# A graph layer on one core: 128 single rows a block, addressed by byte offsets that VectorE works out, and ranges of 38 nodes

## The chip, the cores and the metric

The kernel runs on one core of a Trainium2 chip. The metric is the time of one execution on the device, in microseconds; the time before is the median of three runs, 15436.6 us (15436.29 to 15437.57). The engines are named as the profile names them: PE multiplies matrices (PEld loads its weights), DVE is VectorE, ACT is ScalarE, POOL is GpSimd, SP is SyncE. SP, ACT and POOL also have queues from which transfers (DMAs) are issued.

## What is computed

There are 50000 nodes with 128 numbers each (x), and 1650000 edges (src, dst) sorted by their target dst. Each edge has type 0 or 1. Every node also has an edge to itself. The reference, cut to what matters:

```python
src, dst = (edge_index[0], edge_index[1])
Xs = X[src]
m_data = Xs @ W_data.T + b_data
m_ctrl = Xs @ W_control.T + b_control
msg = jnp.where((edge_types == 0)[:, None], m_data, m_ctrl)
agg = jax.ops.segment_sum(msg, dst, num_segments=X.shape[0])
out = agg + (X @ W_self.T + b_self)
return jax.nn.relu(out)
# around it: x = layernorm(x + the above)
```

So for each edge the row of its source is fetched, and the rows are summed per target and type. The weights can be applied after the sums.

## The kernel before

The edges are cut into blocks. A block is Q = 4 steps, and a step has R = 7 chunks of CH = 128 edges and F = 22 edges more; behind the four steps stand X = 96 edges. A block therefore holds BE = 28 x 128 + 4 x 22 + 96 = 3768 edges, and there are NBLK = 438 blocks. Ten blocks (GB) form a group, for which `load_edges` (line 106) loads the edge lists.

The rows of the sources come in three ways:

- Chunks. Each of the 28 chunks of a block is one gather issued from POOL (line 408): an indirect DMA that fetches 128 rows of x by 128 indices. Its target is one of 70 buffers (`gat`). DVE works out the indices in `fill`, five blocks ahead.
- Left-out edges. The edges of nodes to themselves need no gather, since a window of 128 rows of x is loaded per block anyway (`window`). `fill` takes 22 of them out of each step and puts the 22 extra edges in their places in the chunks, so these ride along. The `left_out` functions add the rows that were taken out.
- Single rows. The X last edges of a block are fetched one by one, each by a DMA of 512 bytes. `single_rows` (line 383) issues a quarter of them after each step: half from SP's queue, half from ACT's. The node's number is loaded from one_g into a register of the queue (line 391), and the DMA addresses x by it (line 396). This happens two blocks ahead (AHEAD); the tile yx has four buffers. All X rows together are the last, shorter chunk of the block.

For each chunk, PE multiplies the gathered rows with a matrix of zeros and ones (`oh`, built by `onehot`, line 356), which has a column for each of W = 36 nodes and two types: the range of nodes that a step may touch. The result `acc` (line 411) is added by DVE into the block's sums at a position read from a register (`add`, line 418). `counts` sums the columns of `oh` to count the edges for the biases. `take_over` (line 424) copies what the last block left for the nodes of this one, on ACT. `layer` applies the weights to the sums, `moments` and `store` do the rest; the square root of the variance is on ACT (line 446), and the result goes out on SP's queue (line 455).

The order is written out by hand (line 457 on). Within block b it is: window of b + 3, edge lists of the next group if the block is the second of its group, add of block b - 1's last step, `take_over`, `add_left_out`; then per step the products, and between them layer, moments and store of block b - 1, onehot and counts of block b + 2, fill of block b + 5, and a quarter of the single rows of block b + 2. Each engine works through its part of this in order. ACT's part is short: copy (line 427), square root (line 446), then its 48 rows.

DMAs of SP and ACT take eight semaphores in turn. Each waits until the DMA that used its semaphore before, from either queue, has landed; this wait is in the DMA instruction itself.

If a step's range were longer than W, or fewer than F edges of a step led from a node to itself, a general path (line 542) would compute everything anew.

Of the kernel before, what the change touches and what calls it, by code (L numbers as in the profile page):

```python
# [11 lines left out]
F32 = mybir.dt.float32  # L12
BF16 = mybir.dt.bfloat16
I32 = mybir.dt.int32
AF = mybir.ActivationFunctionType
ALU = mybir.AluOpType
AX = mybir.AxisListType
# [3 lines left out]

N = 50000
D = 128
E = 1650000
P = 128
EPS = 1e-5
# [3 lines left out]


R = 7
W = 36
Q = 4
B = 128
C = R * Q
X = 96
C1 = C + 1
F = 22
BE = C * CH + Q * F + X  # L40
NBLK = -(-E // BE)
REST = E - (NBLK - 1) * BE
RCH = -(-REST // CH)
LAST = REST - (RCH - 1) * CH
assert RCH <= C
GB = 10
# [7 lines left out]
U = 35  # L54
CPP = -(-(-(-E // CH) + U) // P)
NCH = CPP * P
# [11 lines left out]
def row_bcast(ap, n=P):  # L68
    return bass.AP(tensor=ap.tensor, offset=ap.offset, ap=[[0, n], *ap.ap])


def straight(ctx, tc, c, x, x_t, src_t, dst_t, etype_t, src_f, dst_f, etype_f, src_x, dst_first, out):
# [13 lines left out]
    nc = tc.nc  # L86
    keep = ctx.enter_context(tc.tile_pool(name="keep", bufs=1))
    keep_ps = ctx.enter_context(tc.tile_pool(name="keep_ps", bufs=1, space=bass.MemoryType.PSUM))
    eds = ctx.enter_context(tc.tile_pool(name="eds", bufs=2))
# [11 lines left out]
    stats = keep.tile([P, 2, 2, GROUPS], F32, name="stats")  # L101
    loops = keep.tile([P, GROUPS], F32, name="loops")

    one_s = {}

    def load_edges(g):
        t = eds.tile([1, GB * X], I32, name="one_g")
        nc.sync.dma_start(t, src_x[None, g * GB * X:(g + 1) * GB * X])
        one_s[g] = t
        loads[g] = {}  # L110
        for name, a in (("s", src_t), ("d", dst_t), ("t", etype_t)):
            t = eds.tile([P, GB, C1], I32, name=name, bufs=1)
            nc.sync.dma_start(t.rearrange("p b c -> p (b c)"), a[:, g * GC:(g + 1) * GC])
            loads[g][name] = t
        for name, a in (("sf", src_f), ("df", dst_f), ("tf", etype_f)):
            t = eds.tile([P, GB, Q, F], I32, name=name, bufs=1)
            nc.sync.dma_start(t.rearrange("p b q f -> p (b q f)"),
                              row_bcast(a[g * GB * Q * F:(g + 1) * GB * Q * F]))
            loads[g][name] = t


    load_edges(0)
    BL = TBL
    first_i = keep.tile([P, BL, Q], I32, name="first_i")
    nc.sync.dma_start(first_i.rearrange("p b q -> p (b q)"), row_bcast(dst_first))
# [5 lines left out]
    nc.vector.tensor_tensor(begin, first_i, base.to_broadcast([P, BL, Q]), op=ALU.subtract)  # L131
    nc.vector.tensor_scalar(begin, begin, 0.0, float(B - W), op0=ALU.max, op1=ALU.min)
    place_i = keep.tile([1, BL, Q], I32, name="place_i")
    nc.vector.tensor_copy(place_i, begin[0:1, :, :])
    nc.vector.tensor_tensor(begin, begin, base.to_broadcast([P, BL, Q]), op=ALU.add)
    base_i = keep.tile([1, BL], I32, name="base_i")
    nc.vector.tensor_copy(base_i, base[0:1, :, 0])
# [6 lines left out]

    num = keep.tile([P, 2 * W], F32, name="num")
    nc.gpsimd.iota(num, pattern=[[1, 2 * W]], base=0, channel_multiplier=0,
                   allow_small_or_imprecise_dtypes=True)
    FILL = Q * F + C
    small = keep_ps.tile([P, 2 * W + F + 2 * FILL + 2], F32, name="small")
    num_ps, rank_no_ps = small[:, :2 * W], small[:, 2 * W:2 * W + F]  # L150
    lists = [small[:, 2 * W + F + i * FILL:][:, :FILL] for i in range(2)]
    sums_at = [small[:Q * F, 2 * W + F + 2 * FILL + i:][:, :1] for i in range(2)]
# [16 lines left out]
    for t in range(2):  # L169
        nc.vector.memset(to_row[:, t, t:t + 1], 1.0)  # L170
    bias = keep.tile([3, D], F32, name="bias")
    for i, b in enumerate((c["b_data"], c["b_ctrl"], c["b_self"])):
# [86 lines left out]
    def fill(b):  # L259
# [19 lines left out]
        v = fil.tile([P, C], F32, name="v_new")  # L279
        nc.vector.tensor_reduce(v, new, AX.X, ALU.add)  # L280
        vi = fil.tile([P, C], I32, name="vi")
# [9 lines left out]
        with nc.allow_low_precision(reason="whole numbers below 256, one of them not 0"):  # L291
            nc.vector.tensor_reduce(by, old.rearrange("p (q r) f -> p q f r", r=R), AX.X, ALU.add)  # L292
        bys[b] = by
# [42 lines left out]
    def steps_of(b):  # L336
        return [q for q in range(Q) if len(chunks_of(b, q))]
# [4 lines left out]
    ohs, cnts, ys, accs, xws, xTs, pos, hs, mvs, sds = {}, {}, {}, {}, {}, {}, {}, {}, {}, {}  # L342

    def base_of(b):
        return nc.values_load(base_i[0:1, b:b + 1], engines=[SP], min_val=0, max_val=N - B,
                              skip_runtime_bounds_check_because="it was clamped to this")

    def window(b):
        at = base_of(b)
        xw = stp.tile([B, D], F32, name="xw", bufs=5)  # L350
        nc.sync.dma_start(xw, x[bass.ds(at, B), :])
# [12 lines left out]
    def counts(b):  # L364

        cnt = ohp.tile([P, Q, 2 * W], BF16, name="cnt")
        with nc.allow_low_precision(reason="whole numbers up to R + 1"):
            whole = [q for q in range(Q) if len(chunks_of(b, q)) == R]
            n = len(whole)
            nc.vector.tensor_reduce(cnt[:, :n, :], ohs[b][:, :n * R, :].rearrange("p (q r) w -> p q w r", r=R),  # L370
                                    AX.X, ALU.add)
            for q in steps_of(b):
# [5 lines left out]

    SHARE = X // 2
    TURN = SHARE // Q  # L380
    RANGE = dict(min_val=0, max_val=N - 1, skip_runtime_bounds_check_because="a node's number")

    def single_rows(b, q):

        if q == 0:
            ys[b] = stp.tile([X, D], F32, name="yx", bufs=AHEAD + 2)
        g, i = divmod(b, GB)
        both = []
        for j, (eng, dma) in enumerate(((SP, nc.sync), (ACT, nc.scalar))):
            at = j * SHARE + q * TURN  # L390
            _, nodes = nc.values_load_multi_w_load_instructions(
                one_s[g][0:1, i * X + at:i * X + at + TURN], engines=[eng], **RANGE)
            both.append([(dma, at + k, node) for k, node in enumerate(nodes)])
        for pair in zip(*both):
            for dma, row, node in pair:
                dma.dma_start(ys[b][row:row + 1, :], x[bass.ds(node, 1), :])  # L396

    def products(b, q):
        g, i = divmod(b, GB)
# [2 lines left out]
        for k in ks:  # L402
            if k == C:
                r, y = X, ys.pop(b)
            else:
                r = LAST if b == NBLK - 1 and k == RCH - 1 else P
                y = gat.tile([P, D], F32, name="y")
                nc.gpsimd.indirect_dma_start(  # L408
# [20 lines left out]
    def layer(b):  # L429
        a = sums[b % RING]  # L430
        po = ps_o.tile([B, D], F32, name="po")
        nc.tensor.matmul(po, xTs.pop(b), c["wselfT"], start=True, stop=False)  # L432
        nc.tensor.matmul(po, a[0:3, 2, :B], bias, start=False, stop=False)  # L433
        for t in range(2):
            nc.tensor.matmul(po, a[:, t, :B], c["wmsgT"][:, t * D:(t + 1) * D], start=False, stop=t == 1)  # L435
        pos[b] = po

    def moments(b):
# [6 lines left out]
        sd = stp.tile([B, 1], F32, name="sd")  # L445
        nc.scalar.activation(sd, mv[:, 1:2], AF.Sqrt, bias=c["eps"][:B, :])
        hs[b], mvs[b], sds[b] = h, mv, sd
# [9 lines left out]
    with tc.manual_schedule():  # L457
# [9 lines left out]
        for b in range(AHEAD):  # L467
            for q in range(Q):
                single_rows(b, q)
        left_out_numbers(0)  # L470
        left_out_rows(0)
        for b in range(NBLK + 1):
            if b + 3 < NBLK:
                window(b + 3)
            g, i = divmod(b, GB)
            if i == 1 and g + 1 < GROUPS:
                load_edges(g + 1)
# [7 lines left out]
            for q in range(Q):  # L485
                if q in qs:
                    products(b, q)
                if q == 0 and b > 0:
                    layer(b - 1)
                if q == 1:  # L490
                    left_out_numbers(b + 1)
                if q == 3:
                    left_out_columns(b + RAHEAD)
                if q in qs[:-1]:
                    add(b, q)
                if q == 0 and b > 0:
                    moments(b - 1)
                if q == 0 and b + AHEAD < NBLK:
                    onehot(b + AHEAD)
                if q == 1 and b > 0:  # L500
                    store(b - 1)
                if q == 1 and b + AHEAD < NBLK:
                    counts(b + AHEAD)
                if q == 2:
                    left_out_rows(b + 1)
                    if b + RAHEAD < NBLK:
                        fill(b + RAHEAD)
                if q == 3:
                    left_out_matrix(b + RAHEAD)
                if b + AHEAD < NBLK - 1:  # L510
                    single_rows(b + AHEAD, q)
# [20 lines left out]
    both = keep.tile([3, 1], F32, name="both")  # L532
# [9 lines left out]
def general(ctx, tc, c, x, src, dst, etype, out):  # L542
# [166 lines left out]
    with tc.For_i(0, BGROUPS, 1) as g:  # L709
# [43 lines left out]
        sd = grp.tile([NB, G], F32, name="sd")  # L753
        nc.scalar.activation(sd, mv[:, :, 1], AF.Sqrt, bias=eps[:NB, :])
        rstd = grp.tile([NB, G], F32, name="rstd")
# [8 lines left out]
def gnn_resnorm(  # L764
# [49 lines left out]
    with ExitStack() as own:  # L814
        straight(own, tc, c, x, x_t, src_t, dst_t, etype_t, src_f, dst_f, etype_f, src_x,
                 dst_first, out)
# [49 lines left out]
```

## Time and profile before

| | us |
|---|---|
| median of three runs | 15436.6 |
| profiled execution | 15434.21 |
| its span, first to last instruction | 15432.5 |
| POOL busy | 11631.9 (75%) |
| PE busy | 9551.6 (62%) |
| DVE busy | 7169.3 (46%) |
| ACT busy | 355.9 (2%) |

Busy time leaves out the instructions that set registers, wait or issue DMAs, so ACT's 2% says nothing of its queue. The profile shows the queues as ACTq and SPq. In the groups of the profile, a row gives line, engine, operation, tiles (out<-in), count, busy time, mean duration in ns, idle time before it and what ended this. In the timeline a row gives start, duration, engine, line, operation and, in brackets, the idle time before it. Of one line's instructions the profile lists the shortest, median and longest duration in ns.

### The profile page before, as it was taken

Reading aid. Unit: us, or ns where it says so; the run is one execution under the profiler, and the core shown is the slowest. Engines: PE = TensorE matmul, PEld = TensorE weight load, DVE = VectorE, ACT = ScalarE, POOL = GpSimd, SP = SyncE. Lnnn points to the kernel's source line nnn. Section 1 sums busy time; section 2 is a strip of 40 time slices with the busy share of each in tenths; the row PEclk is TensorE's granted clock in tenths of the full one; section 3 lists DMA queues with packets and bytes.
Section 4 is the critical chain, followed back from the end, with each engine's and each line's share of the span. In section 5 each row is a group of like instructions: output and inputs, shape, how many; then the busy total and the mean of one; then the engine's idle time right before and its main releaser. Section 6 shows DMA issues by size and latency. Waiting matters only on the chain.

```text
span 15432.5 us, 254222 instructions
## 1 busy us (share of the span) xinstructions
PE 9551.6 (62%) x34515; PEld 7418.5 (48%) x34516; DVE 7169.3 (46%) x12518; ACT 355.9 (2%) x881; POOL 11631.9 (75%) x12273
## 2 busy tenths in 40 slices
PE   5666666666666666666666666666666666666666
PEld 4444444444444444444444444444444444444444
DVE  5444444444444444444444444444444444444442
ACT  0000000000000000000000000000000000000000
POOL 6777777777777777777777777777777777777777
DMA  2222222222222222222222222222222222222221
GB/s 67 65 65 69 65 65 65 64 65 65 65 65 67 68 65 65 65 65 65 65 65 65 70 65 65 65 65 65 65 65 65 65 70 65 65 65 65 65 65 57
DMA packets 705933, 1008.97 MB, mean 65 GB/s; under 512 B 263521, under 2 KB 490948, under 8 KB 704222
## 3 DMA queue, kind: packets, MB, share of 16 engines
q0 software_dynamic: 392416, 804.42, 18.3%
q1 hardware_dynamic: 269416, 177.18, 4.0%
q10 hardware_dynamic: 42390, 11.02, 0.3%
q14 instruction: 1426, 11.68, 0.2%
q8 instruction: 285, 4.67, 0.1%
HBM read 962.86 MB, written 28.70 MB: 64 GB/s over the span
## 4 chain that ended last, share of the span: by engine, by line
DMA 69%; issue 11%; POOL 10%; PE 7%; DVE 2%; POOLq 0%; SPq 0%; ACTq 0%; DVEq 0%; ACT 0%
DMA y<-in_x,idx 68%; POOL y L408 10%; PE acc L411 4%; PE po L435 1%; PE po L433 1%; PE po L432 0%; POOLq L408 0%; DMA yx<-in_x 0%; SPq L396 0%; ACTq L396 0%; DVE by L292 0%; PE acc L414 0%; DMA y<-in_x,s 0%; DVE stats L198 0%; DVE stats L199 0%
## 5 line engine op out<-in xcount | busy, mean ns | idle before, releaser
L408 POOL DMA_INDIRECT y<-in_x,idx x12236 | 11605.0, 948 | 3760.9 <-DMA y<-in_x,idx 1973.1
L411 PE MATMUL acc<-oh,y 128*128 128x72 f32 x24526 | 8011.2, 446 | 5293.3 <-DMA y<-in_x,idx 5204.0
L411 PEld LDWEIGHTS acc<-oh,y 128*128 128x128 f32 x24526 | 6050.7, 315 | 7176.0 <-DMA y<-in_x,idx 6659.5
L422 DVE TENSOR_TENSOR sums<-acc,sums 128x108 f32 x1752 | 473.5, 270 | 4399.2 <-PE acc L414 4321.4
L370 DVE TENSOR_REDUCE cnt<-oh 128x216 bf16<-128x1512 f32 x438 | 1238.3, 2827 | 0.1
L360 DVE TENSOR_TENSOR oh<-col,small 128x2088 f32<-128x2088 f32 x438 | 1005.8, 2296 | 0.0
L329 DVE TENSOR_TENSOR sums<-pl,sums 128x384 f32<-128x384 f32 x437 | 243.5, 557 | 1522.8 <-ACT sums L427 1522.8
L414 PEld LDWEIGHTS <-to_row 128*128 128x128 bf16 x3504 | 639.0, 198 | 0.1
L292 DVE TENSOR_REDUCE by<-old 128x88 bf16<-128x616 f32 x437 | 583.2, 1335 | 15.1
L306 DVE COPY at<-small 88x1 f32<-88x1 f32 x437 | 67.5, 154 | 1097.9 <-PE small L299 1083.9
L440 DVE SCALAR_TENSOR_TENSOR h<-po,xw 128x128 f32<-128x128 f32 x438 | 127.5, 291 | 939.1 <-PE po L435 929.7
L435 PE MATMUL po<-wmsgT,sums 128*128 128x128 f32 x1752 | 535.3, 461 | 0.0
L375 DVE TENSOR_REDUCE cnt<-oh 128x72 bf16<-128x576 f32 x438 | 512.7, 1170 | 0.0
L427 ACT COPY sums<-sums 128x384 f32 x437 | 223.9, 512 | 12101.5 <-DMA yx<-in_x 8363.0
L414 PE MATMUL acc<-cnt,to_row 128*128 128x36 bf16 x3504 | 468.9, 217 | 0.0
L435 PEld LDWEIGHTS po<-wmsgT,sums 128*128 128x128 f32 x1752 | 406.1, 322 | 98.3 <-issue 98.3
L299 PE MATMUL small<-ones_b,by 128*88 128x1 bf16 x437 | 94.1, 215 | 493.6 <-DVE by L292 493.6
L276 DVE TENSOR_TENSOR new<-m,small 128x616 f32<-128x616 f32 x437 | 347.5, 795 | 14.9
L273 DVE TENSOR_TENSOR m<-rk,small 128x616 f32<-128x616 f32 x437 | 347.5, 795 | 14.8
L280 DVE TENSOR_REDUCE v_new<-new 128x28 f32<-128x616 f32 x437 | 347.3, 795 | 14.9
L433 PE MATMUL po<-bias,sums 3*128 3x128 f32 x876 | 346.9, 497 | 0.0
L289 DVE TENSOR_TENSOR old<-m,small 128x616 f32<-128x616 f32 x437 | 343.5, 786 | 0.1
(110 smaller groups left out, 3996.0 us busy)
## 6 DMA issues: line engine op xcount, KB each, us to landing
yx<-in_x ACTq DMA_DIRECT2D x20976, 0.5 KB
yx<-in_x SPq DMA_DIRECT2D x20976, 0.5 KB
y<-in_x,idx POOLq DMA_INDIRECT x12236
xw<-in_x SPq DMA_DIRECT2D x438, 64.0 KB
xT<-in_x_t SPq DMA_DIRECT2D x438, 64.0 KB
out<-o SPq DMA_DIRECT2D x438, 64.0 KB
sf<-in_src_f SPq DMA_DIRECT2D x44, 440.0 KB
df<-in_dst_f SPq DMA_DIRECT2D x44, 440.0 KB
```

The source lines that it names most:

```text
L273: nc.vector.tensor_tensor(m, rk_g[g][:, i, :, None].to_broadcast([P, C, F]), rank_no_ps[:, None, :].to_broadcast([P, C, F]), op=ALU.is_equal)
L276: nc.vector.tensor_tensor(new.rearrange("p (q r) f -> p q r f", r=R), m.rearrange("p (q r) f -> p q r f", r=R), vf.rearrange("p (q f) -> p ...
L292: nc.vector.tensor_reduce(by, old.rearrange("p (q r) f -> p q f r", r=R), AX.X, ALU.add)
L360: nc.vector.tensor_tensor(oh[:, :n, :], col_g[g][:, i, :n, None].to_broadcast([P, n, 2 * W]), num_ps[:, None, :].to_broadcast([P, n, 2 * W ...
L370: nc.vector.tensor_reduce(cnt[:, :n, :], ohs[b][:, :n * R, :].rearrange("p (q r) w -> p q w r", r=R), AX.X, ALU.add)
L375: nc.vector.tensor_reduce(cnt[:, q, :], ohs[b][:, k[0]:k[-1] + 1, :].rearrange("p r w -> p w r"), AX.X, ALU.add)
L408: nc.gpsimd.indirect_dma_start(out=y[:r], out_offset=None, in_=x, in_offset=bass.IndirectOffsetOnAxis(ap=idxs[b][:r, k:k + 1], axis=0))
L411: nc.tensor.matmul(acc[:, :2, :].rearrange("p t w -> p (t w)"), y[:r], ohs[b][:r, k, :], start=k == ks[0], stop=k == ks[-1])
L414: nc.tensor.matmul(acc[:, 2, :], to_row[:, t, :], cnts[b][:, q, t * W:(t + 1) * W], start=t == 0, stop=t == 1)
L422: nc.vector.tensor_tensor(part, accs.pop((b, q)), part, op=ALU.add)
L433: nc.tensor.matmul(po, a[0:3, 2, :B], bias, start=False, stop=False)
L435: nc.tensor.matmul(po, a[:, t, :B], c["wmsgT"][:, t * D:(t + 1) * D], start=False, stop=t == 1)
```

## The change

X goes from 96 to 128 and W from 36 to 38. A block then has BE = 3800 edges, and all constants that depend on it follow. The register of a single row no longer holds the node's number but the byte at which its row begins: DVE multiplies the loaded numbers by 512 (at_g), once per group, and both queues load their registers from there. The DMA sees x as one run of bytes and takes 512 from the register's offset. In the built program the queue instruction that stood ahead of each row's DMA (FUSED_REGOPS in the profile) is gone. Each queue now issues 64 rows a block, 16 after each step.

```diff
-W = 36
+W = 38
-X = 96
+X = 128
+U8 = mybir.dt.uint8
+ROW = 4 * D
...
-    one_s = {}
+    at_g = {}
 
     def load_edges(g):
         t = eds.tile([1, GB * X], I32, name="one_g")
         nc.sync.dma_start(t, src_x[None, g * GB * X:(g + 1) * GB * X])
-        one_s[g] = t
+        at = eds.tile([1, GB * X], I32, name="at_g")
+        nc.vector.tensor_scalar(at, t, float(ROW), None, op0=ALU.mult)
+        at_g[g] = at
...
-    RANGE = dict(min_val=0, max_val=N - 1, skip_runtime_bounds_check_because="a node's number")
+    RANGE = dict(min_val=0, max_val=(N - 1) * ROW, skip_runtime_bounds_check_because="where a node's row is")
+    x_bytes = x.rearrange("n d -> (n d)").bitcast(U8)[None, :]
...
-            _, nodes = nc.values_load_multi_w_load_instructions(
-                one_s[g][0:1, i * X + at:i * X + at + TURN], engines=[eng], **RANGE)
-            both.append([(dma, at + k, node) for k, node in enumerate(nodes)])
+            _, rows = nc.values_load_multi_w_load_instructions(
+                at_g[g][0:1, i * X + at:i * X + at + TURN], engines=[eng], **RANGE)
+            both.append([(dma, at + k, row) for k, row in enumerate(rows)])
         for pair in zip(*both):
-            for dma, row, node in pair:
-                dma.dma_start(ys[b][row:row + 1, :], x[bass.ds(node, 1), :])
+            for dma, k, row in pair:
+                dma.dma_start(ys[b][k:k + 1, :].bitcast(U8), x_bytes[:, bass.ds(row, ROW)])
```

## The prediction

> **What bounds the kernel now.** I read the page's chain of waits first, then the costliest groups, then the timeline of POOL, then the queues of ACT and SP, because the change moves work from POOL's gathers to those two queues.
>
> ```profile
> DMA 69%; issue 11%; POOL 10%; PE 7%; DVE 2%; POOLq 0%; SPq 0%; ACTq 0%; DVEq 0%; ACT 0%
> L408 POOL DMA_INDIRECT y<-in_x,idx x12236 | 11605.0, 948 | 3760.9 <-DMA y<-in_x,idx 1973.1
> ```
> ```profile
> 8006.06 0.94 POOL L408 DMA_INDIRECT y<-in_x,idx  x1 [0.30 <-DMA y<-in_x,idx]
> 8007.30 0.94 POOL L408 DMA_INDIRECT y<-in_x,idx  x1 [0.30 <-DMA y<-in_x,idx]
> 8008.55 0.95 POOL L408 DMA_INDIRECT y<-in_x,idx  x1 [0.30 <-DMA y<-in_x,idx]
> 8009.80 0.94 POOL L408 DMA_INDIRECT y<-in_x,idx  x1 [0.30 <-issue]
> ```
>
> The chain names the gathers' DMAs, but the timeline shows a metronome: 0.94 us of gather, 0.30 us of gap, whatever the gap is put down to. A gap that never varies is no wait. POOL issues one gather of 128 rows every 1.2486 us (mean of the undisturbed starts in the trace), and PE, DVE and the landings follow it. The first gather starts at 41.7 us, the last ends at 15413.0, and 19.5 us of tail follow. With the last block's 27 gathers there are 12263: 12263 x 1.2486 = 15312, and 199 stretched ones add 59; with 41.7 and 19.5 that is the span of 15432.5. So the number of gathers sets the time as long as nothing else is slower than a block's 28 x 1.2486 + 0.14 = 35.1 us.
>
> The candidate for "something else" is ACT's queue, which issues half of the single rows:
>
> ```profile
> 8026.30 24.25 ACTq L396 DMA_DIRECT2D yx<-in_x  x48
> 8051.37 0.51 ACT L427 COPY sums<-sums 128x384 f32 x1 [25.82 <-DMA yx<-in_x]
> 8060.16 0.29 ACT L446 ACTIVATE sd<-mv,eps 128x1 f32<-128x1 f32 x1 [8.28 <-DVE mv L444]
> 8061.21 24.10 ACTq L396 DMA_DIRECT2D yx<-in_x  x48
> 8086.17 0.51 ACT L427 COPY sums<-sums 128x384 f32 x1 [25.72 <-DMA yx<-in_x]
> ```
> ```profile
> ACT sums L427 <- DMA yx<-in_x: 8363.0, 315, 34.9
> ```
>
> ACT's block is copy, wait for DVE's moments, square root, 48 rows, copy. Nothing is idle except the 8 us before the square root, and this wait shrinks to 2.9 us (the shortest in the trace) when the copy is late. In 315 blocks of 437 the copy came right behind the rows: ACT is already the last to be ready, with a few us to spare.
>
> ```profile
> L396 ACTq FUSED_REGOPS  x20976: 37/37/37, 3.5 to 15317.2; - x200
> L396 ACTq MOVE yx<-in_x x20976: 29/29/29, 3.5 to 15317.2; - x200
> L396 ACTq DMA_DIRECT2D yx<-in_x x20976: 227/228/628, 3.6 to 15317.3; - x200
> L396 SPq DMA_DIRECT2D yx<-in_x x20976: 224/228/1187, 25.3 to 15313.8; - x200
> ```
> ```profile
> L391 ACTq TENSOR_LOAD <-one_g x1748: 773/1059/1292, 2.4 to 15311.2; - x195
> L425 ACTq TENSOR_LOAD <-shift_i x437: 287/568/752, 87.4 to 15358.8; - x146
> ```
>
> Every row costs three queue instructions: FUSED_REGOPS (node times 512), MOVE, and the DMA. Start to start that is 0.392 us on ACT and 0.41 on SP when nothing holds them (medians of the trace); the means inside a run of rows are about 0.42.
>
> **What the Trainium skill says.** "DMA: Bandwidth & Descriptors", section "SWDGE vs HWDGE vs iDMA": a gather's descriptors are written by software on GpSimd, those of DMAs from SP and ACT by hardware. The trace agrees: 944 ns of POOL for each gather, and rows that leave POOL alone. Same page, "Anatomy of one DMA": about 2.0 us of a DMA are fixed, and a wait on a semaphore is held by the issuing sequencer, not by the DMA engine. The trace shows less, 1.48 us from a row's start to its last landing (mean; 1.18 to 1.78 from 5% to 95%), and the holding. "GPSIMD Engine Reference", "Key points": GpSimd shares its SBUF interfaces with VectorE, so VectorE instructions in a two-port mode or with two SBUF inputs disturb it. The trace agrees: the stretched gathers stand beside such DVE work.
>
> ```profile
> 249.69 0.61 DVE L190 TENSOR_SCALAR col_f<-tf 128x880 f32<-128x880 int32 x1
> 250.34 1.08 DVE L191 TENSOR_TENSOR col_f<-col_f,rel_f 128x880 f32<-128x880 f32 x1
> ```
> ```profile
> 249.44 1.15 POOL L408 DMA_INDIRECT y<-in_x,idx  x1 [0.30 <-DMA y<-in_x,idx]
> 250.89 1.33 POOL L408 DMA_INDIRECT y<-in_x,idx  x1 [0.30 <-DMA y<-in_x,idx]
> ```
>
> **The change, part by part.**
>
> Fewer gathers. A block holds 28 x 128 + 4 x 22 + X edges: 3768 before, 3800 after. 1650000 edges need 438 blocks before (the last with 3384 edges, 27 chunks) and 435 after (the last with 800, 7 chunks). Gathers: 437 x 28 + 27 = 12263, then 434 x 28 + 7 = 12159. The 104 that go are worth 104 x 1.2486 = 129.9 us. The groups of ten stay 44, so the stretched gathers stay.
>
> The multiplication at_g on DVE, 1280 numbers once per group. By L190's row (880 in 0.61 us) it takes about 0.8 us. DVE is busy 7169 of 15432 us, so it costs DVE nothing; on POOL it can stretch a gather as L190 did, by 0.2 us. 43 x 0.2 = 9 us, with 0 and 0.4 us (17 us) as ends.
>
> Its wait. It stands on DVE before the last add of block b-1, and waits for one_g, which SP issues only behind its rows. In the trace before, that load lands about 5 us after this add starts in most groups (issue at 8158.41, add at 8154.08, its landing taken 2 us later, an estimate by the fixed cost in "Anatomy of one DMA"), and over 20 us after it in the first ones. Behind it on DVE stand the add, the take-over's consumer, the moments and so ACT's copy and square root; PE's layer waits for the add. None of this reaches POOL: its 70 gather buffers are 87 us of lead, and PE catches up (0.70 us for two records of a gather against 1.25). It lengthens ACT's block by 4.5 us in ten, 0.45 a block.
>
> Wider ranges. oh, cnt and the sums go from 36 to 38 columns, 5.6% of L360, L370, L375 and L422 (7.4 us a block), 0.4 us on a DVE that has 18 us free a block; PE's matmuls grow by 4 columns of 72 under gaps of half a microsecond. Nothing. In the given inputs the longest range of a step is 34 nodes, so the fallback path does not start.
>
> Rows. 64 instead of 48 per queue and block, without FUSED_REGOPS. Removing it takes 37 ns and its gap, 66 ns: 0.326 us on ACT, 0.34 on SP. But another limit is near: the rows of both queues share 8 semaphores in turn, and each DMA waits until the one 8 places earlier has landed. With rows alternating, a queue has 4 in flight: 1.48 / 4 = 0.37 us, 0.39 with the spread of the landings. Four rows after each register load start freely. ACT's block after, from the rows shown: four quarters, each with 1.63 us between the rows around a register load (1.52 measured, and 4 more registers at (1059 - 568) / 11 = 45 ns, less 66), 0.56 after the first row (0.63 less 66 ns), and 14 pitches p; less the 1.63 counted once too often; plus 1.04 to the copy, 2.9 to the square root, 1.2 to the first row, 0.45 for the new wait: 12.7 + 56 p. It reaches POOL's 35.1 at p = 0.400. With p = 0.326 it is 31.0, with three free rows and eleven at 0.388, p = 0.375, 33.7; with today's 0.434 (mean of all pitches under 0.8 us) 37.0. I take 0.375 plus 0.01 for holds by long loads, 34.3 us: under POOL's, by 0.8 us. SP has 27.4 us of work a block before (a period of 34.5 less a hold of 7.1 around 1060 us) and comes to 34 by the same pitch.
>
> Sum: 15432.5 - 129.9 + 9 = 15311.6 of span. The profiled execution took 15434.21, 1.7 more than its span, and the median is 2.4 above that: 15316 us.
>
> **Rivals.** The queues of ACT and SP become the bound, and the kernel gets slower. Place: the rows of L401; price: each 0.01 us of p above 0.400 costs 0.56 us x 434 = 243 us. At p = 0.415 it gives 15312 + 365 + 4 = 15680; if the byte offsets bring nothing, 0.434, 35.1 becomes 37.0 and the time 16140. For it: the 8 semaphores, the bursts in which the two queues wait for each other, and a DMA in bytes that may take over 228 ns. Against it: p's mean today holds waits of SP for DVE's output that vanish when ACT is late.
>
> A draw: p between 0.403 and 0.408 gives the gain back, 15436 in the middle.
>
> Gathers get dearer because a third more rows share the DMA engines: 0.011 us a gather would eat the gain. Against it: the pitch stays within 1.245 and 1.255 for 90% of the gathers, with and without rows beside them, at a DMA share of 22%. Beyond that point 15460.
>
> **How the numbers follow.** POOL stays the bound: 0.55, 15316 (15298 to 15330 by the ends above). Draw 0.10, queues over the gain 0.33, dearer gathers 0.02. This measurement tells 0.2%, 31 us, from no change. The range reaches from 15298 up to 15700, which leaves out the far half of the slow case, about 0.15, and a few hundredths below. Faster 0.55, same 0.10, slower 0.35.
>
> **What would show it.** Right: 12159 gathers at 1.249 us, no FUSED_REGOPS at the rows, ACT's rows in under 29 us a block, the wait before the square root near 3 us, at_g beside a gather of 1.15 us. Wrong: gathers with gaps of several us before which POOL waits for PE, and PE in turn for DVE or for yx; rows over 30 us a block; a row's DMA above 0.3 us; p above 0.40.

## The result, and the profile after

| | before | after |
|---|---|---|
| median of five runs each, us | 15436.6 | 15346.81 |
| lowest and highest, us | 15436.23, 15437.71 | 15330.1, 15368.69 |
| profiled execution, us | 15434.21 | 15330.1 |
| its span, us | 15432.5 | 15328.1 |
| gathers | 12263 | 12159 |

The ratio of the times is 0.9942, with a 95% interval of 0.9928 to 0.9956: 0.6% faster. The forecast was 15316 us, with a range of 15298 to 15700: of the 120.6 us forecast for the median, 89.8 came.

The page's chain of waits and two of its costliest groups, after, with the second group's row of before (line, engine, operation, tiles, count; busy time and mean ns of one; idle time before it and what ended most of it):

```profile
DMA 41%; issue 17%; ACTq 15%; PE 10%; DVE 8%; SPq 7%; POOL 1%; ACT 1%; DVEq 0%; POOLq 0%
L413 POOL DMA_INDIRECT y<-in_x,idx x12152 | 11544.6, 950 | 3737.1 <-issue 2296.8
L333 DVE TENSOR_TENSOR sums<-pl,sums 128x384 f32<-128x384 f32 x434 | 242.0, 558 | 6378.5 <-ACT sums L432 6378.5
```
```profile
L329 DVE TENSOR_TENSOR sums<-pl,sums 128x384 f32<-128x384 f32 x437 | 243.5, 557 | 1522.8 <-ACT sums L427 1522.8
```

The chain looks different: ACT's and SP's queues, at 0% before, have 22% of it, and by lines the single rows' transfers have 26% and the gathers' 10%, where the gathers' had 68% before. By the chain alone the rows would be the bound now. The gathers say otherwise; they look the same. POOL's idle time is 3737.1 / 12152 = 0.3075 us a gather, against 3760.9 / 12236 = 0.3074 before. So in the mean no gather waited longer than the constant gap, and POOL still sets the length of this execution. The row of L333 is the new fact: DVE's take-over waits 6378 us for ACT's copy, four times the 1523 us of before. ACT has come late, but POOL doesn't notice.

The timeline of ACT and its queue, after:

```profile
8042.87 30.80 ACTq L401 DMA_DIRECT2D yx<-in_x  x64
8074.48 0.51 ACT L432 COPY sums<-sums 128x384 f32 x1 [32.53 <-DMA yx<-in_x]
8076.74 0.30 ACT L451 ACTIVATE sd<-mv,eps 128x1 f32<-128x1 f32 x1 [1.75 <-DVE mv L449]
8077.97 30.87 ACTq L401 DMA_DIRECT2D yx<-in_x  x64
8109.65 0.51 ACT L432 COPY sums<-sums 128x384 f32 x1 [32.61 <-PE acc L416]
```

Copy to copy is 35.17 us, and POOL's block is 35.1. 64 rows take 30.8 us where 48 took 24.2. In 93% of the blocks the square root now follows the copy within 2.5 us, mostly at the shortest distance, 2.26 us: ACT has no slack left in its block. Its mean period over the whole execution is 35.09 us, POOL's 35.15.

The instructions of the rows, after (shortest, median and longest ns; first and last start in us):

```profile
L401 ACTq MOVE yx<-in_x x27776: 29/29/30, 6.5 to 15245.9; - x200
L401 ACTq DMA_DIRECT2D yx<-in_x x27776: 227/228/558, 6.5 to 15246.0; - x200
```
```profile
L396 ACTq TENSOR_LOAD <-at_g x1736: 1023/1297/1584, 5.2 to 15239.2; - x193
```

FUSED_REGOPS is gone from the rows, and a DMA addressed in bytes takes the same 228 ns. The median pitch of ACT's rows fell from 0.392 to 0.326 us. Loading 16 registers takes 1297 ns where 12 took 1059.

Who waits for whom, after, and PE's wait for gathers before (engine and line, what it waited for: us in total, times, longest us):

```profile
ACT sums L432 <- DMA yx<-in_x: 9724.7, 300, 36.8
DVE sums L333 <- ACT sums L432: 6378.5, 433, 22.4
...
PE acc L416 <- DMA y<-in_x,idx: 2807.7, 4989, 2.1
...
PE pl L319 <- DVE sums L333: 1724.1, 315, 15.4
```
```profile
PE acc L411 <- DMA y<-in_x,idx: 5204.0, 8983, 4.1
```

PE waited 5204 us for gathers before, 2808 us now: it comes to them later, held by DVE, which is held by ACT. That lateness is what the gather buffers take up, and they aren't used up: by the ends of PE's products and the starts of the gathers, the buffer that a gather took had been free for at least 43.6 us (before: 55.7).

Account of the span on POOL, from the starts of all gathers in the two traces:

| | us |
|---|---|
| 104 gathers fewer, at 1.2486 | -129.9 |
| stretched gathers: 199 with 59.7 us over, now 240 with 77.8 | +18.1 |
| undisturbed pitch, 1.2486 to 1.2488 | +2.6 |
| first gather later, 41.67 to 42.25 | +0.6 |
| tail behind the last gather, 19.5 to 23.7 | +4.2 |
| sum, and the difference of the spans | -104.4 |

The median of five is 16.7 us above the profiled execution, and the five spread over 38.6 us where the kernel before spread over 1.5. No trace holds that part.

### The profile page after: what moved, and what is told of

Same layout as the page of the kernel before. It is cut to its first block, busy times and chain, and to the rows that moved or that the text cites. A ratio compares the mean times of both kernels' runs of the same rounds, so it can differ in the third digit from the quotient of the medians.

```text
span 15328.1 us, 238434 instructions
## 1 busy us (share of the span) xinstructions
PE 8510.5 (56%) x34235; PEld 7111.3 (46%) x34236; DVE 7169.5 (47%) x12480; ACT 353.8 (2%) x875; POOL 11552.7 (75%) x12169
## 3 DMA queue, kind: packets, MB, share of 16 engines
q0 software_dynamic: 389088, 797.58, 20.6%
## 4 chain that ended last, share of the span: by engine, by line
DMA 41%; issue 17%; ACTq 15%; PE 10%; DVE 8%; SPq 7%; POOL 1%; ACT 1%; DVEq 0%; POOLq 0%
DMA yx<-in_x 26%; ACTq L401 11%; DMA y<-in_x,idx 10%; PE acc L416 7%; SPq L401 6%; ACTq L396 3%; DMA out<-o 2%; DMA xT<-in_x_t 1%; POOL y L413 1%; DMA xw<-in_x 1%; DVE sums L333 1%; ACT sums L432 1%; PE po L440 1%; ACTq L430 1%; PE po L438 1%
## 5 line engine op out<-in xcount | busy, mean ns | idle before, releaser
L413 POOL DMA_INDIRECT y<-in_x,idx x12152 | 11544.6, 950 | 3737.1 <-issue 2296.8
L416 PE MATMUL acc<-oh,y 128*128 128x76 f32 x24318 | 6971.0, 437 | 2855.2 <-DMA y<-in_x,idx 2807.7
L416 PEld LDWEIGHTS acc<-oh,y 128*128 128x128 f32 x24318 | 5741.7, 322 | 3939.6 <-DMA y<-in_x,idx 3730.9
L333 DVE TENSOR_TENSOR sums<-pl,sums 128x384 f32<-128x384 f32 x434 | 242.0, 558 | 6378.5 <-ACT sums L432 6378.5
L374 DVE TENSOR_REDUCE cnt<-oh 128x228 bf16<-128x1596 f32 (+1 forms) x435 | 1274.7, 2930 | 0.1
L319 PE MATMUL pl<-z,ones_b 88*128 88x256 bf16 x434 | 169.8, 391 | 1802.8 <-DVE sums L333 1724.1
L364 DVE TENSOR_TENSOR oh<-col,small 128x2204 f32<-128x2204 f32 (+1 forms) x435 | 1050.0, 2414 | 0.0
L303 PEld LDWEIGHTS <-by 128*88 128x88 bf16 x434 | 65.6, 151 | 1583.0 <-DVE by L296 1582.4
L427 DVE TENSOR_TENSOR sums<-acc,sums 128x114 f32 x1737 | 473.7, 273 | 330.9 <-PE acc L419 226.4
L296 DVE TENSOR_REDUCE by<-old 128x88 bf16<-128x616 f32 x434 | 579.3, 1335 | 14.9
L379 DVE TENSOR_REDUCE cnt<-oh 128x76 bf16<-128x608 f32 x434 | 504.5, 1162 | 0.0
L419 PE MATMUL acc<-cnt,to_row 128*128 128x38 bf16 x3474 | 473.3, 220 | 0.0
L438 PEld LDWEIGHTS po<-bias,sums 3*128 3x128 f32 x870 | 216.3, 308 | 531.5 <-DVE sums L427 443.1
```

Of the source, the lines that this page charges most:

```text
L364: nc.vector.tensor_tensor(oh[:, :n, :], col_g[g][:, i, :n, None].to_broadcast([P, n, 2 * W]), num_ps[:, None, :].to_broadcast([P, n, 2 * W ...
L379: nc.vector.tensor_reduce(cnt[:, q, :], ohs[b][:, k[0]:k[-1] + 1, :].rearrange("p r w -> p w r"), AX.X, ALU.add)
L413: nc.gpsimd.indirect_dma_start(out=y[:r], out_offset=None, in_=x, in_offset=bass.IndirectOffsetOnAxis(ap=idxs[b][:r, k:k + 1], axis=0))
L416: nc.tensor.matmul(acc[:, :2, :].rearrange("p t w -> p (t w)"), y[:r], ohs[b][:r, k, :], start=k == ks[0], stop=k == ks[-1])
L419: nc.tensor.matmul(acc[:, 2, :], to_row[:, t, :], cnts[b][:, q, t * W:(t + 1) * W], start=t == 0, stop=t == 1)
L427: nc.vector.tensor_tensor(part, accs.pop((b, q)), part, op=ALU.add)
```

## The experiments

All experiments ran on three other chips: e1 to e7 on the one numbered 11, e8 to e11 on 9, e12 on 7. There the kernel before takes 22282 to 22299 us, not 15437, so each kernel is compared only with the runs of before beside it. The times expected in e1 to e4, and the sides of e5 to e7 for a before of 15437 us, are for the first chip and can't be tested with these. What the experiments settle is how the parts of the change weigh where the queues bind. The account above rests on the two traces of the first chip; no experiment took a part of the change away there. Where Q stands in an expectation, it is the theory that the queues of SP and ACT decide; G has dearer gathers instead, and M slower memory.

| label | what differs | us | ratio to before, 95% interval | us a block |
|---|---|---|---|---|
| e1_again, e5_again | nothing (the kernel after) | 22307, 22356 | 1.003 [1.002, 1.004] | 51.4 |
| e2_one_op, e6_one_op | no copy on ACT (but in the last block) | 22759, 22767 | 1.022 [1.019, 1.024]; 1.021 [1.018, 1.023] | 52.3 |
| e3_late_mult | at_g four blocks later | 22197 | 0.996 [0.995, 0.998] | 51.0 |
| e4_by_node, e7_by_node | 128 rows, by node number | 25616, 25618 | 1.150 [1.148, 1.151]; 1.150 [1.147, 1.152] | 58.9 |
| e9_bytes_alone | 96 rows, W = 36, by byte | 19989 | 0.897 [0.895, 0.898] | 45.6 |
| e10_rows_64 | 64 rows, by byte | 18538 | 0.831 [0.830, 0.833] | 41.9 |
| e11_rows_40 | 40 rows, by byte | 18290 | 0.821 [0.819, 0.822] | 41.1 |
| e12_wide_alone | 96 rows, by node, W = 38 | 22230 | 0.998 [0.996, 0.999] | 50.8 |

The block counts for the last column are 438 with 96 rows, 435 with 128, 442 with 64 and 445 with 40. The kernel before has 22283 / 438 = 50.9 us.

### The same kernels on the other chips: e1, e5, e8

No edit: e1 and e5 are the kernel after, e8 is the kernel before.

> The changed kernel unaltered, for a second profile beside the first (15330.1 us, the fastest of its five runs of 15330 to 15369). Theory Q (the queues of ACT and SP have become a second bound, as slow a block as POOL): in a slower execution ACT's copy is further behind the block's first gather at the end than the 21 us of the first profile, by about as much as the time is longer, and POOL's pitch is the same 1.249 us. Theory G (the gathers have become dearer, the queues cost nothing): the longer time shows as more or longer stretched gathers than the 240 of the first profile, and ACT's distance at the end is the same.

> The changed kernel unaltered once more, since in the last four runs even the kernel before took 22284 us: ACT's and SP's queues show stretches there in which each instruction takes 0.7 us. Where before takes 15437 us again: 15330 to 15370 us. Theory Q (queues a second bound): ACT's copy is further behind the block's first gather at the end than the 21 us of the first profile, by about as much as the time is longer than 15330, with POOL's pitch 1.249 us. Theory G (gathers dearer): more or longer stretched gathers than 240, the same distance. Where before takes 22284 again: 22300, whatever the theory.

> The kernel before unaltered, for its profile on the chip of the last runs, where it takes 22299 us instead of 15437. Theory Q (there the queues of ACT and SP bound every kernel, before too): queue instructions of 0.7 us as in e1, POOL waiting for PE between its gathers, and PE for DVE or ACT; ACT's rows take longer than 40 us a block. Theory M (memory or gathers are slower there): POOL's gathers or the landings are longer than in the first profile of before, queue instructions are not.

Measured: 22307 us (one run), 22356 us (22320 to 22419, 14 runs) and 22264 us (one run). The gain of the first chip is gone: 0.3% slower. POOL's row in e8, the costliest groups:

```profile
L408 POOL DMA_INDIRECT y<-in_x,idx x12236 | 11603.2, 948 | 10531.7 <-PE acc L411 5573.8
```

A gather takes the same 948 ns as on the first chip, but POOL idles 10532 us instead of 3761, mostly for PE. The waits of e8 show who holds PE:

```profile
ACT sums L427 <- DMA yx<-in_x: 18655.1, 379, 193.8
DVE sums L329 <- ACT sums L427: 12135.3, 409, 51.3
...
PE pl L315 <- DVE sums L329: 10125.1, 396, 37.5
POOL y L408 <- PE acc L411: 5586.0, 1330, 17.5
```

Read upwards from the last row: POOL waits for PE (a gather buffer to come free), PE for DVE's take-over, DVE for ACT's copy, and that stands behind ACT's rows (their issue is counted in the first row). The same chain, with these names, holds in the kernel after there (e1): DVE for ACT 10540 us, PE for DVE 8827, POOL for PE 5612. This is the prediction's rival "the queues become the bound", reached already by the kernel before. Theory M finds no support: besides the gathers' 948 ns, the gathers' DMA packets of 4096 bytes last 211 ns in the median in both traces of before, and the packets that bring instructions 438 and 448. Why the queues are slow there stands in the instructions of one line, here e1's rows:

```profile
L401 ACTq MOVE yx<-in_x x27776: 2/29/1422, 6.3 to 22255.6; - x200
L401 ACTq DMA_DIRECT2D yx<-in_x x27776: 2/228/1462, 6.3 to 22255.7; - x200
L401 SPq MOVE yx<-in_x x27776: 1/29/1509, 26.0 to 22251.0; - x200
```

The medians are those of the first chip; the shortest and longest aren't. In stretches, instructions of a queue follow one another at 0.70, 1.4 or 2.1 us, whatever they are. In e1, 5263 of ACT's 27778 MOVEs and 13271 of SP's 29085 take other than 25 to 45 ns; on the first chip none does, before or after. ACT's timeline in e1 shows what it does to a block:

```profile
8053.20 45.15 ACTq L401 DMA_DIRECT2D yx<-in_x  x64
8099.16 0.51 ACT L432 COPY sums<-sums 128x384 f32 x1 [46.88 <-DMA xT<-in_x_t]
8101.42 0.29 ACT L451 ACTIVATE sd<-mv,eps 128x1 f32<-128x1 f32 x1 [1.75 <-DVE mv L449]
8102.63 33.68 ACTq L401 DMA_DIRECT2D yx<-in_x  x64
```

64 rows take 45 us in one block and 34 in the next, where the first chip has 31.

### One part alone: e4, e7, e9, e12

e4 and e7 keep the addressing by node with 128 rows and ranges of 38; e9 has the byte offsets with 96 rows and ranges of 36; e12 has only the wider ranges. Against the kernel before (e4, e12) and after (e9):

```diff
e4, e7:
-W = 36
+W = 38
-X = 96
+X = 128
e12:
-W = 36
+W = 38
e9:
-W = 38
+W = 36
-X = 128
+X = 96
```

> 128 single rows and ranges of 38 nodes, but the rows addressed by the node's number as before, with the register instruction ahead of every DMA. Theory Q: ACT's block gets longer by 0.045 us (the difference of the mean pitches, 0.434 less 0.389) to 0.066 us for each of some 60 rows, 2.5 to 4 us, and exceeds POOL's by this: 16340 to 17000 us. Theory G: the queues are off the path, and without the multiplication that stretches gathers the time is 15436.6 - 130, 15307 us.

> As e4: 128 single rows addressed by node, with the register instruction. Where before takes 15437 us, theory Q: 16340 to 17000 us (2.5 to 4 us more a block than POOL); theory G: 15307 us.

> X and W as before (96 and 36), byte offsets alone. Theory Q: from the three kernels measured where before takes 22299 us (50.9, 51.3 and 58.9 us a block with 144, 128 and 192 queue instructions for 48, 64 and 64 rows) an instruction costs 0.117 us, a row 0.148 us more and the rest of a block 27 us: 48 x (2 x 0.117 + 0.148) + 27 = 45.3 us, 438 blocks 19840 us. Theory G or M: no change but the multiplication's 18 us, 22320 us. Where before takes 15437: 15450 to 15455 us by both, from the stretched gathers.

> The kernel before with ranges of 38 nodes and nothing else: 96 rows, addressed by node. It takes the third part of the change by itself. Theory Q (the wider ranges cost nothing, as the prediction has it: their 0.4 us of DVE a block and 4 more columns a matmul lie beside the gathers on the first chip and beside the row queues here): the time of the kernel before on the same chip, ratio 0.998 to 1.002. Rival (on a chip where PE and DVE are waited for, wider tiles lie on the path: 0.4 us of DVE and 28 matmuls 4 columns wider, together 0.5 to 1 us a block of 438): 22480 to 22720 us, ratio 1.010 to 1.020. If on a chip like the first one (before at 15437 us): Q 15436, ratio 1.000.

Measured: 15.0% slower for the rows without byte offsets, 10.3% faster for byte offsets without the rows (19989 us, where theory Q had 19840), and 0.25% faster (0.15 to 0.36%) for the wider ranges alone. Per block and with 96 rows, byte offsets save 50.87 - 45.64 = 5.2 us, which is 0.11 us for each of 48 instructions taken off a queue; with 128 rows 58.9 - 51.4 = 7.5 us, 0.12 us for each of 64. An instruction and its gap cost 66 ns on the first chip. 16 more rows a queue cost 51.39 - 45.64 = 5.7 us with byte offsets and 8.0 by node number. (e5 and e9 ran on two chips, on which before differs by 0.1%.) So the change takes 5.2 us off a block there and puts 5.7 on, and the saving of three blocks in 438 (0.7%) just doesn't pay for it. POOL's row in e9, in the costliest groups, beside e8's above:

```profile
L413 POOL DMA_INDIRECT y<-in_x,idx x12236 | 11603.5, 948 | 8278.6 <-PE acc L416 3088.9
```

The same 12236 gathers with the same busy time, and 2253 us less idle time. The spans differ by 22262.1 - 19997.6 = 2264.5 us: nearly all of it is waiting that POOL no longer does. The wider ranges cost nothing that can be measured, as the prediction had it; the 52 us on the good side aren't explained.

### Less on the queues: e10, e11

The kernel after with fewer rows; nothing else is edited.

```diff
-X = 128
+X = 64
```

(and 40 in e11.)

> The changed kernel with 64 single rows a block instead of 128: 442 blocks. Theory Q where before takes 22299 us: 32 x 0.382 + 27 = 39.2 us a block, 17330 us, so fewer single rows are much faster there. Theory G or M: more gathers, hence slower than the changed kernel by 1.2%, 22620 us. Where before takes 15437: 441 x 28 + 19 = 12367 gathers, 12367 x 1.2488 + 78 + 62 = 15584 us.

> The changed kernel with 40 single rows a block: 445 blocks, 444 x 28 + 15 = 12447 gathers. Theory Q where before takes 22299 us: 20 x 0.382 + 27 = 34.6 us of queue work a block, just under POOL's 35.1, so POOL's even pitch of 1.249 us returns and the time is 12447 x 1.2488 + 78 + 62 = 15684 us, as it would be on any chip. Theory G or M: 22800 us.

Measured: 18538 and 18290 us, slower than theory Q expected by 1208 and 2606 us. Taking rows off pays less and less: 0.36 us a row and queue from 128 to 96, (45.6 - 41.9) / 16 = 0.23 from 96 to 64, (41.9 - 41.1) / 12 = 0.07 from 64 to 40. The expectations took over the first price and POOL's even pitch from the first chip. The starts of the gathers show which of them fails:

```
distance from one gather to the next:   over 5 us        2 to 5 us        under 1.3 us
before there (e8)                       439, 5192 us     1306, 3666 us     9925
by node, 128 rows (e4)                  468, 8744 us     1282, 3550 us     9924
after there (e1)                        436, 5328 us     1283, 3666 us     9898
bytes alone, 96 rows (e9)               249, 2368 us     1408, 4113 us    10021
64 rows (e10)                            72,  474 us     1419, 4232 us    10327
40 rows (e11)                            31,  203 us     1280, 3911 us    10554
```

The long pauses go with the rows: they are the waits for the queues. In e8, 434 of the 439 end 0.27 us after PE is through with the buffer that the gather takes. The short ones, some 1300 of 2 to 5 us in every kernel, stay whatever the rows are, and on the first chip there are one or two. They aren't waits for a buffer: in e11 it had been free for over 1 us in 1273 of 1280, for 15 us in the median. In e11 they cost 3911 - 1280 x 1.249 = 2313 us over the pitch, of the 2640 us by which that kernel exceeds an even pitch of its 12447 gathers. POOL's timeline in e11:

```profile
9004.97 0.95 POOL L413 DMA_INDIRECT y<-in_x,idx  x1 [0.30 <-issue]
9008.99 0.94 POOL L413 DMA_INDIRECT y<-in_x,idx  x1 [3.07 <-remote]
9010.24 0.94 POOL L413 DMA_INDIRECT y<-in_x,idx  x1 [0.31 <-issue]
```

The second gather starts after a gap of 3.07 us instead of 0.30, and the profile names no releaser on this core. In some 880 of e11's 1280 short pauses it names a PE step, but the free buffers speak against that. With 40 rows ACT has time again, as its first wait in the list shows (the square root waits for DVE, not the copy for rows):

```profile
ACT sd L451 <- DVE mv L449: 5089.0, 380, 21.6
```

So there is a second bound at about 41 us a block: POOL with its own interruptions, whose cause is open. 40 rows with byte offsets is the fastest version of those run there, 17.9% below before. On the first chip it can't win while POOL is the bound: it has 12447 gathers against 12159, 288 x 1.2488 = 360 us more. That is worked out and wasn't run there.

### The place of the multiplication: e3

at_g is made at the sixth block of the group before instead of the second, when its data have long arrived.

```diff
+    def offsets(g):
+        at = eds.tile([1, GB * X], I32, name="at_g")
+        nc.vector.tensor_scalar(at, one_s.pop(g), float(ROW), None, op0=ALU.mult)
+        at_g[g] = at
...
+    offsets(0)
...
-        at = eds.tile([1, GB * X], I32, name="at_g")
-        nc.vector.tensor_scalar(at, t, float(ROW), None, op0=ALU.mult)
-        at_g[g] = at
+        one_s[g] = t
...
+            if i == 5 and g + 1 < GROUPS:
+                offsets(g + 1)
```

> The multiplication by 512 is moved from the second block of a group to the sixth, where its load landed long ago, so DVE no longer waits for it (648 us over 44 times in the changed kernel). Theory Q: ACT's block gets shorter by up to 0.45 us on average, its lag is gone sooner, 15325 to 15340 us. Theory G, or if the wait is hidden by DVE's free time: no change, 15347 us with its spread.

Measured: 22197 us, against 22307 and 22356 for the kernel after there. The waits of e1, and then of e3:

```profile
DVE at_g L112 <- DMA one_g<-in_src_x: 1075.9, 44, 45.1
```
```profile
DVE at_g L110 <- DMA one_g<-in_src_x: 1.2, 1, 1.2
```

DVE's wait of 24 us in each group of ten blocks is gone, and the profiled spans differ by 22305.6 - 22151.7 = 154 us, 3.5 us a group. By the medians, 22307 and 22356 against 22197, it is 2.5 to 3.6 us a group. So the wait is on the path where ACT is late: behind it stand DVE's moments, and behind those ACT's square root and rows. On the first chip the wait is 647.8 us in 44 times, and POOL's row above shows that none of it reached a gather.

### The take-over without ACT: e2, e6

The copy on ACT and DVE's addition after it become one addition on DVE, so that nothing on DVE waits for ACT's copy.

```diff
+    def take_over_and_add_left_out(b):
+        at = nc.values_load(shift_i[0:1, b:b + 1], engines=[DVE], min_val=0, max_val=B,
+                            skip_runtime_bounds_check_because="it was clamped to this")
+        part, old = sums[b % RING][:, :, :B], sums[(b - 1) % RING][:, :, bass.ds(at, B)]
+        nc.vector.tensor_tensor(part, pls.pop(b)[:, :, :B], old, op=ALU.add)
...
-                if b < NBLK:
+                if b < NBLK - 1:
+                    take_over_and_add_left_out(b)
+                elif b < NBLK:
                     take_over(b)
-            if b < NBLK:
+            if b == 0:
                 add_left_out(b)
```

> take_over and add_left_out become one addition on DVE (the old sums read at their shift, the left-out part from PSUM), so ACT has no copy and DVE no wait for it. Theory Q: ACT's block loses the copy, its register load and the way there, 2 to 3 us, and falls to about 32.5 us against POOL's 35.1; what lag there is goes, the time falls to 15325 us (12159 gathers at 1.2488 and 240 stretched ones with 78 us, 42 ahead and 20 behind) and five runs differ by under 6 us. Theory G: 15347 us and a spread of 40 us, as in the changed kernel.

> As e2: take_over and add_left_out as one addition on DVE. Where before takes 15437 us, theory Q: 15325 us, runs within 6 us of each other; theory G: 15347 us with a spread of 40 us. The run e2 tells that the wait for ACT may come back at another place, DVE's wait for the square root: then the time lies between.

Measured: 2.2 and 2.1% slower than before, 1.8 to 2.0% slower than after. The waits of e2:

```profile
PE small L303 <- DVE by L296: 8968.5, 302, 54.9
...
DVE rstd L463 <- ACT sd L457: 5063.7, 200, 51.6
```

The wait moved instead of going. DVE now stops one step later, at `store`, for ACT's square root, which stands behind the same rows. What DVE has behind it there, the match matrices and indices that PE needs, waits with it: PE's wait for L296 is 8968 us where e1 has 2441. Neither theory of e2 had this, and e6's expectation had the place but not that it is slower. DVE still needs ACT in every block, so taking one of two such steps away freed nothing. Why it costs 2% more than the kernel after isn't settled.

## Why the prediction was right

- Fewer gathers: right. 12159 of them at 1.2488 us, -129.9 us, is the whole of the gain, and POOL's idle time a gather is unchanged to 0.2 ns. The gain is shown for the traced execution, the fastest of the five.
- at_g's stretching of gathers: the mechanism right, the size too small. The prediction had 43 x 0.2 = 9 us with 17 as the upper end; stretching grew by 18.1 us. The multiplication stretches its gather in 40 of 44 groups, by 0.30 us on average, 13 us in all. The term was taken from a gather beside L190; the other 5 us came beside the older pairs of DVE work on the columns. The multiplication took 815 ns, as predicted. DVE's and POOL's timelines of the kernel after:

```profile
473.01 0.82 DVE L112 TENSOR_SCALAR at_g<-one_g 1x1280 int32<-1x1280 int32 x1 [17.43 <-DMA one_g<-in_src_x]
```
```profile
471.83 0.94 POOL L413 DMA_INDIRECT y<-in_x,idx  x1 [0.30 <-issue]
473.08 1.56 POOL L413 DMA_INDIRECT y<-in_x,idx  x1 [0.30 <-issue]
474.95 0.94 POOL L413 DMA_INDIRECT y<-in_x,idx  x1 [0.30 <-DMA y<-in_x,idx]
```

One gather, among the longest of these, takes 1.56 us where its neighbours take 0.94, and it is under way together with at_g. This agrees with the Trainium skill, "GPSIMD Engine Reference", section "8. Key points", which has the two engines share their SBUF interfaces. The section names VectorE instructions in a two-port mode or with two SBUF inputs; at_g has one input, and no run shows in which mode it works. The size is the trace's.
- at_g's wait: right that it reaches no gather on the first chip. Wrong that it lengthens ACT's block there by 0.45 us: the copy follows the last row by 1.06 us in the mean and the square root the copy by 2.31, together 0.06 over their medians. e3 shows what it costs where ACT is late, about 3 us a group. The 4.5 us in ten blocks of the prediction is near that.
- Wider ranges, nothing: e12 agrees, on another chip.
- Rows: FUSED_REGOPS and its gap gave the 66 ns, and the DMA stayed at 228. ACT's block was put at 34.3 us, 0.8 under POOL's; it is 35.09, less than 0.1 under. The rows take 30.5 us from first to last in the mean: over the 29 that were to show the step right, and over the 30 that were to show it wrong. In the terms of the sum, the 14 pitches p of a quarter are 0.401 us in the mean, where it used 0.375 and 0.01, and where 0.400 was its turning point. (All pitches under 0.8 us have 0.389, but two longer ones a block are left out of that.) The rows around a register load are 1.88 us apart instead of 1.63, and the first pitch is 0.60 instead of 0.56. Together that is 1.8 us too little; 0.6 too much stood in the square root, 2.31 us behind the copy instead of 2.9, and 0.45 in at_g's wait. So it was in part luck that ACT stayed under POOL's pace. A row's latency rose too, from 1.48 to 1.59 us, so the limit of eight semaphores that the step reckons with moved up; no run tests this limit by itself. "The queues become the bound", with a chance of 0.33, was nearer than the sum of 34.3 says.
- What the lateness did: ACT's copy begins about 50 us behind the first gather of its block near the start, and about 21 us at the end (before: 5 to 10). It falls up to block 200, to about 19 us, with ACT's blocks at 35.02 us in the mean; after that they are 35.14, POOL's pace, and it falls no further. What slows them there isn't shown. It stays inside the 87 us of lead that 70 buffers give.
- Dearer gathers: their DMA packets did last longer, 251 ns in the mean against 221, and their share of the 16 engines rose from 18.3 to 20.6%; POOL's pitch stayed, so this reached nothing. It doesn't follow the number of rows: on the other chips too, 40, 64 and 96 rows give 220 to 221 ns and 128 give 250. The cause is open.
- The sum: 15311.6 of span predicted, 15328.1 measured. Of the 16.5 us, 9.1 are the stretching, 2.6 the pitch, 0.6 the start and 4.2 the tail, which the prediction left as it was. Its narrow range, 15298 to 15330, doesn't follow from the ends that it names: 0 and 17 us of stretching give 15307 to 15324. The median of 15346.8 lies outside both; it lies in the wide range, which was drawn for the slower cases.
- The median: put at 4.4 us over the span, it is 18.7 over. The growth of the spread from 1.5 to 38.6 us would fit a queue that in some executions passes POOL's pace for a while. This stays open: only the trace of one of the five, the shortest, was kept, and no experiment ran on that chip.

The result holds for the chip that it was measured on. On the three others the rival's mechanism rules before the change as well as after (the kernel before was traced on one of them, the kernel after on another), and on the one where the kernel after ran it brings nothing.

## What to carry to other kernels

Compare each queue's period of work with that of the engine that sets the pace, and count the small instructions in it: work may be moved to a queue until the periods meet, and at that point a profile can still show an untouched bound while the lead of its buffers is being used; here 43.6 of 87 us were left at the least. Drop the instructions that a queue spends on addresses before adding transfers to it; here each was worth 66 ns where nothing was disturbed, and 110 to 120 ns on the slower chips. When an engine waits for another in two places, removing one of them alone can move the wait to the second, as in e2.

## What the runs showed of the hardware that was not expected

- The same kernel takes 15437 us on one chip and 22282 to 22299 on three others, at a granted TensorE clock of 1.000 and with gathers of the same 948 ns. In the traces of those chips, queue instructions come at steps of 0.70 us in stretches: in e1, 3899 steps of 0.67 to 0.73 us on ACT (2773 us in all) and 7955 on SP (5656 us), against 166 and 211 in the kernel after on the first chip. POOL pauses some 1300 times for 1 to 4 us although a buffer is free, and PE, in e11, 2079 times for up to 3.3 us with no releaser. What holds the instructions wasn't found, nor is it shown that the chip itself makes the difference: the first result has no chip's number.
- There the best split between gathers and single rows is another one: with byte offsets, 40 rows a block beat 96 by 8.5% and 128 by 18%.
- A DVE operation on a single partition, 815 ns long, stretches a concurrent gather by 0.30 us on average, at an overlap of 0.66 us.
- A queue loads 16 registers in 1.30 us on ACT and 1.21 on SP, 12 in 1.06 and 0.99, one in 0.57.
